# Layer 0's normed input and softmax weights transposed through memory, reads issued when their write has landed

## The chip, the cores and the metric

One core of one Trainium2 chip runs the whole program; the other cores are idle. The metric is the device time of one execution in microseconds (us). The engines of the core are TensorE (PE, with its weight loads listed as PEld), VectorE (DVE), ScalarE (ACT), GpSimd (POOL) and SyncE (SP), which here only issues DMAs. The time before is 4961.98 us, the median of three runs (4956.65 to 4962.49).

## The reference, cut to what matters

Four layers work on `x` of 64 graphs, 256 nodes each, 128 features, all with one 256x256 matrix `adj`. Each layer adds its output to `x`. The change is almost wholly in layer 0:

```python
h = jnp.maximum(_layernorm(x, axis=-1), 0.0)       # 64 graphs x 256 nodes x 128
W1, W2 = adj[:, :128], adj[:, 128:]
s1 = jnp.einsum('bkf,ef->bke', h, W1)              # receivers
s2 = jnp.einsum('bkf,ef->bke', h, W2)              # senders
pre = s1[:, :, None, :] + s2[:, None, :, :] + b_lin
hh = jnp.where(pre >= 0, pre, 0.2 * pre)           # 64 x 256 x 256 x 256 values
e = jnp.einsum('bije,e->bij', hh, a) + adj
attn = jax.nn.softmax(e, axis=2)
x = x + jax.nn.sigmoid(jnp.einsum('bij,bjf->bif', attn, h))
```

Layers 1 to 3 are much smaller: a gated aggregation over `adj` (layer 1), an attention with a tanh and an exponential (layer 2), and five steps of a gated recurrent update (layer 3), which multiply 256x256 by 256x128 and 128x128 by 128x256 per graph.

## The kernel before, in words

**Tiling.** The 64 graphs are cut into 34 groups (line 15): 1, 1, thirty groups of 2, 1, 1. A block is 128 nodes, so a group of two graphs has G = 4 blocks and a tile of it is 128 partitions x 512 values. Everything is float32.

**Layer 0's pairs.** For every graph, receiver i and feature e the kernel needs the maximum of a sender row and a number of the receiver. `Pairs.make` (line 681) writes these in tiles `r` of 4 x 2 x 256 values (one batch: 8 receivers, 128 features, 256 senders). Three engines share the batches: ACT (line 720) and POOL (line 725) make one 128x256 piece an instruction, DVE (line 702) a whole batch (128x2048) or half of one (128x1024). PE multiplies a batch by a window of weights (line 786) into the graph's scores `e_ps`: four matmuls of 512 columns for a batch of the first kind, eight of 256 columns for one of the second. When at least SPARE = 5 batches wait for PE, DVE adds the second half of the features to a batch in place (`merge`, line 744). Two merged batches take 8 such additions and spare PE one batch.

**Order.** The order of all engines is written when the program is built. A planner (line 1359 on) keeps a clock for PE, DVE, ACT and POOL (`Model`), adds a cost for each recorded instruction, and always records next what can start first. Chains of steps (`Chain`, line 1273) hold the rest of the layers as generators: each `yield` names the engine of the next step, a condition and an earliest time; `paced` chains are also held to one step per `pace` ns. Engines then run their instructions in the recorded order and wait for each other by semaphores.

**Transposes.** Matmuls need some tiles with features on partitions. Layers 1 to 3 send most of them through memory: `crossed` (line 97) records on SP's queue a write of the tile to DRAM and at once a read back in transposed order, 16 bytes at a time (4 values, one per block); the read waits for the write's landing. The planner holds the user of the tile back by `Model.transfer`: TURN = 12500 ns of a serial memory, plus SURE = 7000 ns. Such tiles are laid out as [feature, node, block] (`across`). A few late tiles are transposed by PE (`by_pe`, line 875).

**Layer 0's own transposes.** `head` (line 528) norms a group's `x` (`ln_relu`, line 448), and `transpose_blocks` (line 483) turns it: G transposes on PE and one copy on ACT (line 493) into `h0t`. From `h0t` come `s1` and `s1n` (receivers, lines 545 and 547), a bound through a small DMA round trip (`bounds`, line 552), and per graph `left_ps` and `s2` (`senders`, line 577) and the opening matmul of the scores (`open`, line 750). When a graph's scores are complete, `softmax0` (line 791) takes the row maximum on DVE, the exponential with its row sum on ACT (line 809; the sum is read out by a second instruction of ACT), the reciprocal on DVE (line 815), four transposes of the weights on PE (line 819 on), one copy of them on ACT with a factor 0.5 (line 826), the matmul with `h` (line 831), two tanh on ACT (line 839) and an addition to `x` on DVE.

**SP's queue** takes, in recorded order: the loads of `x` (line 149), the writes and reads of `crossed` (lines 101 and 103), the rows and the bound (lines 571 and 573) and the stores of the result (line 1267).

Of the kernel before, what the change touches and what calls it, by code (L numbers as in the profile page):

```python
# [12 lines left out]
P = 128  # L13
# [11 lines left out]
TURN = 12500  # L25
# [16 lines left out]
class Model:  # L42
# [16 lines left out]
    def transfer(self, e):  # L59

        self.memory = max(self.memory, self.t[e] + 900) + TURN
        return self.memory + SURE
# [3 lines left out]
def kernel(ctx: ExitStack, tc: tile.TileContext, ins: dict, out: bass.AP):  # L66
# [30 lines left out]
    def crossed(src, tag, name, by, bufs=1):  # L97

        shape = [P, src.shape[1], src.shape[2]]
        there = dp.tile(shape, F32, tag="there%d" % src.shape[2], name="there", bufs=3)  # L100
        nc.sync.dma_start(out=there, in_=src)
        t = bp.tile(shape, F32, tag=tag, name=name, bufs=bufs)
        nc.sync.dma_start(out=t, in_=there.rearrange("p f g -> f p g"))
        return t, model.transfer(by)
# [67 lines left out]
    adj_n = fetch([P, 2, N], "adj_n", adj.rearrange("(c p) m -> p c m", p=P), nc.scalar)  # L172
# [66 lines left out]
    def constants0():  # L239
# [125 lines left out]
        dve(1).tensor_copy(left_b, p[:, P + 1 : P + 2])  # L365
        counts["left"] += 1
# [81 lines left out]
    def ln_relu(space, xt, tag, ln, when=None, at=None, across=False):  # L448
# [22 lines left out]
        for g in range(G):  # L471
            if g % 2 == 0:
                yield "act"
            if g == 0:
                shape = [P, P, G] if across else [P, G, P]
                h = space.tile(shape, F32, tag=ln, name=tag, bufs={ap: 3, bp: 1}.get(space))
            act(P, 2, 1).activation(  # L477
                h[:, :, g] if across else h[:, g, :], xt[:, g, :], AF.Relu, bias=shift[:, g : g + 1],
                scale=rstd[:, g : g + 1],
            )  # L480
        return h

    def transpose_blocks(space, src, name, banks, when=None, tag=None, bufs=None):

        yield "pe", when
        G, _, W = sizes(src)
        tp = banks([P, G, P], name + "_ps")
        turn()
        for g in range(G):
            tr(tp[:, g, :], src[:, g, :])  # L490
        yield "act"
        t = space.tile([P, G, P], F32, tag=tag or name, name=name, bufs=bufs)
        act(W).copy(t, tp)  # L493
        return t


    def first_head(xt, to, snd):
# [3 lines left out]
        h_t = yield from transpose_blocks(ap, h, "h0t", psum_h)  # L501
# [50 lines left out]
    def bounds(of):  # L552
# [4 lines left out]
        G = h_t.shape[1]  # L557
        p = psum_h([P, P], "bound_ps")
        model.op("pe", P * 1.676)
        for c in range(G):  # L560
            nc.tensor.matmul(
                p[bass.ts(c, 32), :], lhsT=left_w, rhs=h_t[:, c, :], start=True, stop=True
# [14 lines left out]
    def senders(b, of, to):  # L577

        h_t = flat(of["h_t"][:, 2 * b : 2 * b + 2, :])
        if "bound" not in of:  # L580
# [3 lines left out]
        mm(p, lhsT=left2, rhs=h_t, start=True, stop=True)  # L584
# [3 lines left out]
            adj_l, p, of["bound"][:, 2 * b : 2 * b + 1], adj_n[:, 0, :], ALU.min, ALU.add  # L588
# [6 lines left out]
        for ec in range(2):  # L595
            mm(p[:, ec, :], lhsT=w_p[:, 1, bass.ts(ec, P)], rhs=h_t, start=True, stop=True)
# [5 lines left out]
    class Pairs:  # L602
# [5 lines left out]
        def __init__(self, g, b, of, snd):  # L608
# [8 lines left out]
            self.s1n_v = of["s1n"][:, :, bass.ts(b, N)].rearrange(  # L617
                "p c (k g t) -> p c g k t", k=2, g=4
            )
            self.s1n_b = of["s1n"][:, :, bass.ts(b, N)].rearrange(  # L620
                "p c (k g t) -> p c k g t", k=2, g=4
            )
# [49 lines left out]

        def nodes(self, batch, g2):
# [3 lines left out]
                (g, k, self.b * N + 32 * g + t + (P + k if two else k * P))  # L677
# [3 lines left out]
        def make(self, who):  # L681
# [10 lines left out]
            if who == "dve":  # L692
# [4 lines left out]
                if batch["two"]:  # L697
                    s1n = self.s1n_b[:, ec, 1, 2 * g2 : 2 * g2 + n, t : t + 2].unsqueeze(3)
# [92 lines left out]
    def softmax0(g, b, of, e_ps, snd):  # L791
# [27 lines left out]
        for jc in range(2):  # L819
            for ic in range(2):  # L820
                tr(
                    pt_ps[:, jc, bass.ts(ic, P)], pm[:, ic, bass.ts(jc, P)]
                )
# [50 lines left out]

    def by_pe(h, tag, bufs=None, when=None, space=bp):

# [595 lines left out]
```

## Time and profile before

| what | value |
|---|---|
| runs | 4956.65, 4961.98, 4962.49 us |
| profiled execution | 4962.75 us, of which the profile's span is 4960.9 us |
| PE busy | 4923.5 us (99%) |
| ACT busy | 4873.2 us (98%) |
| DVE busy | 4841.8 us (98%) |
| POOL busy | 4756.8 us (96%) |
| granted TensorE clock | 0.999 |
| DMA queue of SP | 121.35 MB in 3429712 packets, 56.5% of 16 engines' time |
| transposes through memory of 256 KB | 104 (`hf`) + 86 (`h`), each a write and a read |

"Busy" is the time in which at least one instruction of the engine is under way. Instructions overlap on PE and ACT, so their cost is read from the distance between the starts (or ends) of neighbours rather than from the duration of one. The list of groups gives, for each line and form, the number of instructions, the busy time of the group, and the mean duration of one. A matmul of the program stands as two instructions in the profile. The DMA share in the view by windows is a sum over packets and can exceed 1 (1.82 is seen).

### The profile page before, as it was taken

Reading aid. Unit: us, or ns where it says so; the run is one execution under the profiler, and the core shown is the slowest. Engines: PE = TensorE matmul, PEld = TensorE weight load, DVE = VectorE, ACT = ScalarE, POOL = GpSimd, SP = SyncE. Lnnn points to the kernel's source line nnn. Section 1 sums busy time; section 2 is a strip of 40 time slices with the busy share of each in tenths; the row PEclk is TensorE's granted clock in tenths of the full one; section 3 lists DMA queues with packets and bytes.
Section 4 is the critical chain, followed back from the end, with each engine's and each line's share of the span. In section 5 each row is a group of like instructions: output and inputs, shape, how many; then the busy total and the mean of one; then the engine's idle time right before and its main releaser. Section 6 shows DMA issues by size and latency. Waiting matters only on the chain.

```text
span 4960.9 us, 176723 instructions
## 1 busy us (share of the span) xinstructions
PE 4923.5 (99%) x69735; PEld 2389.7 (48%) x69735; DVE 4841.8 (98%) x8229; ACT 4873.2 (98%) x12812; POOL 4756.8 (96%) x10545
## 2 busy tenths in 40 slices
PE   9999999999999999999999999999999999999998
PEld 4454545554454544444445444444454444444444
DVE  9999999999999999999999999999999999999994
ACT  8999999999999999999999999999999999999994
POOL 8999999999999999999999999999999999999981
PEclk9999999999999999999999999999999999999999
DMA  0357576777676776866757656656666555542310
GB/s 21 10 17 23 25 30 27 32 32 30 30 33 27 32 32 28 34 27 30 33 27 30 30 27 32 32 26 32 30 32 32 26 31 30 29 26 12 19 9 8
DMA packets 3431090, 132.92 MB, mean 27 GB/s; under 512 B 3369201, under 2 KB 3405937, under 8 KB 3430257
## 3 DMA queue, kind: packets, MB, share of 16 engines
q1 hardware_dynamic: 3429712, 121.35, 56.5%
q8 instruction: 547, 8.96, 0.9%
q14 instruction: 287, 2.34, 0.3%
q10 hardware_dynamic: 544, 0.26, 0.0%
HBM read 61.48 MB, written 60.10 MB: 25 GB/s over the span
## 4 chain that ended last, share of the span: by engine, by line
PE 85%; ACT 7%; DVE 5%; POOL 1%; issue 1%; DMA 0%; ACTq 0%; DVEq 0%; POOLq 0%
PE e_ps L786 53%; PE gate_ps L128 8%; PE hv_ps L128 5%; ACT r L720 5%; PE m_ps L128 5%; PE s_ps L128 3%; DVE r L702 3%; PE o_ps L128 2%; PE e_ps L128 2%; PE rc_ps L128 1%; POOL r L725 1%; PE rsum_ps L128 1%; DVE r L744 1%; PE e_ps L135 1%; PE th_ps L128 1%
## 5 line engine op out<-in xcount | busy, mean ns | idle before, releaser
L725 POOL TENSOR_SCALAR r<-s,s1n 128x256 f32<-128x256 f32 x9920 | 4509.6, 543 | 47.1 <-PE e_ps L786 21.1
L720 ACT ACTIVATE r<-s_act,s 128x256 f32<-128x256 f32 x9768 | 4421.0, 1212 | 1.1 <-PE e_ps L786 1.0
L786 PE MATMUL e_ps<-r,a_win 128*32 128x256 f32 (+1 forms) x41040 | 3323.2, 464 | 9.1 <-DVE r L702 7.5
L702 DVE TENSOR_TENSOR r<-s_ps,s1n 128x2048 f32<-128x2048 f32 (+1 forms) x1367 | 2417.3, 1804 | 0.0
L786 PEld LDWEIGHTS e_ps<-r,a_win 128*32 128x32 f32 x41040 | 1394.2, 110 | 1603.7 <-issue 825.0
L744 DVE SCALAR_TENSOR_TENSOR r<-s_ps,s1n,r 128x256 f32<-128x256 f32 x4056 | 1671.5, 472 | 0.8 <-POOL r L725 0.3
L477 ACT ACTIVATE h<-xt,bsh,brs 128x128 f32<-128x128 f32 x512 | 417.6, 1318 | 7.5 <-POOL bsh L470 7.5
L720 ACT ACTIVATE r<-s,s 128x256 f32<-128x256 f32 x512 | 319.2, 1416 | 0.0
L128 PE MATMUL m_ps<-adj_q,hn 128*32 128x256 f32 x4096 | 252.1, 380 | 1.6 <-ACT hn L1140 1.6
L128 PEld LDWEIGHTS m_ps<-adj_q,hn 128*32 128x32 f32 x4096 | 160.8, 132 | 89.4 <-issue 25.4
L1192 ACT ACTIVATE gate_ps<-gate_ps,bz 128x512 f32<-128x512 f32 (+1 forms) x140 | 202.5, 1447 | 0.0
L1194 ACT ACTIVATE hv_ps<-hv_ps,bh 128x512 f32<-128x512 f32 (+1 forms) x140 | 200.9, 1435 | 0.0
L1180 ACT ACTIVATE m_ps<-gate_ps,br 128x512 f32<-128x512 f32 (+1 forms) x140 | 194.0, 1386 | 0.0
L1176 ACT COPY m_t<-m_ps 128x512 f32<-128x512 f32 (+1 forms) x140 | 184.7, 1319 | 0.0
L128 PE MATMUL gate_ps<-m_t,t_w_w 128*32 128x512 f32 (+1 forms) x1360 | 174.8, 568 | 0.4 <-ACT m_t L1090 0.3
L128 PE MATMUL hv_ps<-rh,u_th 128*32 128x512 f32 (+1 forms) x1360 | 170.9, 567 | 1.3 <-DVE rh L1103 1.3
L128 PE MATMUL gate_ps<-m_t,w_t 128*32 128x512 f32 (+1 forms) x1360 | 171.1, 568 | 0.6 <-ACT m_ps L1100 0.6
L128 PE MATMUL hv_ps<-m_t,t_w_w 128*32 128x512 f32 (+1 forms) x1360 | 171.0, 567 | 0.0
L809 ACT ACTIVATE pm<-e_ps,nmax 128x256 f32<-128x256 f32 x128 | 145.7, 1138 | 2.4 <-DVE nmax L800 2.4
L128 PE MATMUL gate_ps<-hf,u_t 128*32 128x512 f32 (+1 forms) x1088 | 139.8, 567 | 0.0
L128 PE MATMUL s_ps<-h0t,w_p 128*32 128x256 f32 (+1 forms) x1568 | 138.9, 445 | 0.6 <-ACT h0t L493 0.5
L940 ACT ACTIVATE th_ps<-th_ps,a_src 128x256 f32<-128x256 f32 x128 | 134.8, 1053 | 1.5 <-PE th_ps L128 1.5
(223 smaller groups left out, 4612.8 us busy)
## 6 DMA issues: line engine op xcount, KB each, us to landing
there<-hf SPq DMA_DIRECT2D x104, 256.0 KB
hn<-there SPq DMA_DIRECT2D x104, 256.0 KB
there<-h SPq DMA_DIRECT2D x86, 256.0 KB
h_t<-there SPq DMA_DIRECT2D x60, 256.0 KB
xt<-in_x_dram SPq DMA_DIRECT2D x30, 256.0 KB
out_dram<-xt SPq DMA_DIRECT2D x30, 256.0 KB
h3t<-there SPq DMA_DIRECT2D x26, 256.0 KB
row<-rows SPq DMA_DIRECT2D x128, 0.5 KB
```

The source lines that it names most:

```text
L128: nc.tensor.matmul(out[bass.ts(c, 32)], lhsT=lhsT[:, bass.ts(c, 32)], rhs=rhs, **flags)
L477: act(P, 2, 1).activation(h[:, :, g] if across else h[:, g, :], xt[:, g, :], AF.Relu, bias=shift[:, g : g + 1], scale=rstd[:, g : g + 1],)
L702: nc.vector.tensor_tensor(r[:, 2 * g2 : 2 * g2 + n, :, :], s2[:, ec : ec + 1, :].unsqueeze(1).to_broadcast([P, n, 2, N]), s1n.to_broadcast ...
L720: nc.scalar.activation(r[:, g, ic, :], s2[:, ec, :], AF.Relu, bias=s1[:, ec, i : i + 1])
L725: nc.gpsimd.tensor_scalar(r[:, g, ic, :], s2[:, ec, :], FLT_MAX, s1n[:, ec, i : i + 1], ALU.min, ALU.max,)
L744: nc.vector.scalar_tensor_tensor(r[:, g, ic, :], self.own("dve")[:, 1, :], self.of["s1n"][:, 1, i : i + 1], r[:, g, ic, :], ALU.max, ALU.add,)
L786: nc.tensor.matmul(to, lhsT=a_win[:, sign, 31 - t : 63 - t], rhs=of, start=False, stop=self.over, skip_group_check=True,)
L809: act(N, 1, more=119).activation(pm[:, ic, :], e_ps[:, ic, :], AF.Exp, bias=nmax[:, ic : ic + 1], scale=-1.0, accum_out=rs[:, ic : ic + 1],)
L1176: act(W).copy(m_t, m_ps)
L1180: act(W, 1).activation(m_ps, g_ps, AF.Tanh, bias=br, scale=0.5)
L1192: act(W, 1).activation(g_ps, g_ps, AF.Tanh, bias=bz, scale=0.5)
L1194: act(W, 1).activation(hv_ps, hv_ps, AF.Tanh, bias=bh)
```

## The change

`h0t` and the softmax weights `pt` are now made by `crossed`, which can put its tile in another pool. `h0t` goes through memory for every group but the first, `pt` for all graphs of groups 0 to 31 (62 of 64). `crossed` records the write and leaves the read in a list; the planner records the read when its own clock has reached the write's landing (LANDED = 2700 ns after the write's turn) and only then knows when the tile is due (FETCH = 10300 ns of the serial memory, and SURE as before).

All tiles of `h` now have the layout [feature, node, block], and with it `h0t`, `s1`, `s1n` and the weights: a graph of a group of two takes two of every four values. The exponential's two halves are written with every second value each (`pm`), without a row sum. `h` has a 129th column of 2.0, set on POOL, so that the weights' matmul yields twice the row sum beside the weighted sum; the reciprocal is taken of that after the matmul, and the factor 0.5 falls away. The columns of `adj` that are added to the scores are kept in the matching order (`adj_j`). The planner also gets other places for the last layer's exclusive use of two banks (`Home.enter` and `leave`, step by step instead of for the whole layer), a pace of 1700 instead of 2300 for the two lanes of layer 3, and a `due` that is raised when a step is looked at rather than when it is queued.

```diff
...
 MEMORY = (7000, 30000)
-TURN = 12500
+STORE = 1300
+LANDED = 2700
+FETCH = 10300
 SURE = 7000
...
-        self.memory = max(self.memory, self.t[e] + 900) + TURN
+        self.memory = max(self.memory, self.t[e] + 900) + STORE
+        return self.memory + LANDED - STORE
+    def fetch(self, landed):
+        self.memory = max(self.memory, landed) + FETCH
         return self.memory + SURE
...
-    def crossed(src, tag, name, by, bufs=1):
-        shape = [P, src.shape[1], src.shape[2]]
+    def crossed(src, tag, name, by, bufs=1, space=bp):
+        shape = [P, P, src.shape[2]]
         there = dp.tile(shape, F32, tag="there%d" % src.shape[2], name="there", bufs=3)
-        nc.sync.dma_start(out=there, in_=src)
-        t = bp.tile(shape, F32, tag=tag, name=name, bufs=bufs)
-        nc.sync.dma_start(out=t, in_=there.rearrange("p f g -> f p g"))
-        return t, model.transfer(by)
+        nc.sync.dma_start(out=there, in_=src[:, 0:P, :])
+        t = space.tile(shape, F32, tag=tag, name=name, bufs=bufs)
+        due = [None]
+        landed = model.transfer(by)
+        def read():
+            nc.sync.dma_start(out=t, in_=there.rearrange("p f g -> f p g"))
+            due[0] = model.fetch(landed)
+        reads.append((landed, read))
+        return t, due
...
     a_col = column("L0_gnn_a", nc.scalar)
-    adj_n = fetch([P, 2, N], "adj_n", adj.rearrange("(c p) m -> p c m", p=P), nc.scalar)
+    adj_n = bp.tile([P, 2, N], F32, tag="e_t", name="adj_n", bufs=2)
+    fetch([P, 2, N], "adj_n", adj.rearrange("(c p) m -> p c m", p=P), nc.scalar, adj_n)
+    adj_j = constant([P, 2, P, 2], "adj_j")
+    by_j = adj_j.rearrange("p c q m -> p c (q m)")
     blin = column("L0_gnn_b_lin")
...
         dve(1).tensor_copy(left_b, p[:, P + 1 : P + 2])
+        dve(2 * N).tensor_copy(
+            adj_j.rearrange("p c q m -> p c m q"), adj_n.rearrange("p c (m q) -> p c m q", m=2)
+        )
         counts["left"] += 1
...
             if g == 0:
-                shape = [P, P, G] if across else [P, G, P]
-                h = space.tile(shape, F32, tag=ln, name=tag, bufs={ap: 3, bp: 1}.get(space))
+                wide = P + 1 if space is ap else P
+                h = space.tile([P, wide, G], F32, tag=ln, name=tag, bufs={ap: 3, bp: 1}.get(space))
             act(P, 2, 1).activation(
-                h[:, :, g] if across else h[:, g, :], xt[:, g, :], AF.Relu, bias=shift[:, g : g + 1],
+                h[:, 0:P, g], xt[:, g, :], AF.Relu, bias=shift[:, g : g + 1],
                 scale=rstd[:, g : g + 1],
             )
+        if space is ap:
+            pool(80).memset(h[:, P : P + 1, :], 2.0)
         return h
-    def transpose_blocks(space, src, name, banks, when=None, tag=None, bufs=None):
+    def by_pe(h, tag, bufs=None, when=None, space=bp, banks=None):
         yield "pe", when
-        G, _, W = sizes(src)
-        tp = banks([P, G, P], name + "_ps")
+        if when is free_a:
+            using_a.append(tag)
+        G = h.shape[2]
+        tp = (banks or psum_a)([P, P, G], "h_t_ps")
         turn()
         for g in range(G):
-            tr(tp[:, g, :], src[:, g, :])
+            tr(tp[:, :, g], h[:, 0:P, g])
         yield "act"
-        t = space.tile([P, G, P], F32, tag=tag or name, name=name, bufs=bufs)
-        act(W).copy(t, tp)
+        t = space.tile([P, P, G], F32, tag=tag, name="h_t", bufs=bufs)
+        act(P * G).copy(t, tp)
         return t
+    def free_a():
+        return not using_a
...
         h = yield from ln_relu(ap, xt, "h0", "h0", at=LANDS)
-        h_t = yield from transpose_blocks(ap, h, "h0t", psum_h)
+        h_t = yield from by_pe(h, "h0t", None, None, ap, psum_h)
         to.update(h=h, h_t=h_t)
...
         h = yield from ln_relu(ap, xt, "h0", "h0")
-        h_t = yield from transpose_blocks(ap, h, "h0t", psum_h, settled)
+        h_t, at = crossed(h, "h0t", "h0t", "act", None, ap)
         to.update(h=h, h_t=h_t)
+        yield "pe", None, at
         if counts["left"] > 0:
...
-        h_t = flat(of["h_t"][:, 2 * b : 2 * b + 2, :])
+        h_t = of["h_t"][:, :, 2 * b : 2 * b + 2]
         if "bound" not in of:
...
         p = psum_h([P, N], "left_ps")
-        mm(p, lhsT=left2, rhs=h_t, start=True, stop=True)
+        mm(pairs(p), lhsT=left2, rhs=h_t, start=True, stop=True)
         yield "dve", None, of["bound_at"]
...
         dve(N, 1).scalar_tensor_tensor(
-            adj_l, p, of["bound"][:, 2 * b : 2 * b + 1], adj_n[:, 0, :], ALU.min, ALU.add
+            adj_l, p, of["bound"][:, 2 * b : 2 * b + 1], by_j[:, 0, :], ALU.min, ALU.add
         )
...
+        def at(self, q, k):
+            return q * self.of["h_t"].shape[2] + 2 * self.b + k
         def nodes(self, batch, g2):
...
             return [
-                (g, k, self.b * N + 32 * g + t + (P + k if two else k * P))
+                (g, k, self.at(32 * g + t + (k if two else 0), 1 if two else k))
                 for g in (2 * g2, 2 * g2 + 1) for k in range(2)
...
                 mm(
-                    self.e_ps[:, ic, :], lhsT=v2_rep,
-                    rhs=flat(self.of["h_t"][:, 2 * b : 2 * b + 2, :]),
+                    pairs(self.e_ps[:, ic, :]), lhsT=v2_rep,
+                    rhs=self.of["h_t"][:, :, 2 * b : 2 * b + 2],
                     start=(ic == 0), stop=False, skip_group_check=True,
...
             dve(N, more=10).tensor_tensor_reduce(
-                e_ps[:, ic, :], e_ps[:, ic, :], adj_n[:, 1, :] if ic else snd["adj_l"], -1.0, FLT_MAX,
+                e_ps[:, ic, :], e_ps[:, ic, :], by_j[:, 1, :] if ic else snd["adj_l"], -1.0, FLT_MAX,
                 ALU.add, ALU.min, nmax[:, ic : ic + 1],
...
             if ic == 0:
-                pm = ap.tile([P, 2, N], F32, tag="pm", name="pm", bufs=1)
-                rs = sp.tile([P, 2], F32, tag="rs", name="rs")
-            act(N, 1, more=119).activation(
-                pm[:, ic, :], e_ps[:, ic, :], AF.Exp, bias=nmax[:, ic : ic + 1], scale=-1.0,
-                accum_out=rs[:, ic : ic + 1],
-            )
-        yield "dve"
-        rh = sp.tile([P, 2], F32, tag="rh", name="rh")
-        dve(2).reciprocal(rh, rs)
-        yield "pe"
-        pt_ps = e_ps
-        turn()
-        for jc in range(2):
-            for ic in range(2):
-                tr(
-                    pt_ps[:, jc, bass.ts(ic, P)], pm[:, ic, bass.ts(jc, P)]
-                )
-        yield "act"
-        pt = ap.tile([P, 2, N], F32, tag="pt", name="pt", bufs=1)
-        act(2 * N, table=1).activation(pt, pt_ps, AF.Copy, scale=0.5)
-        yield "pe"
-        o_ps = e_ps[:, :, 0:P]
+                pm = ap.tile([P, P, 2, 2], F32, tag="pm", name="pm", bufs=1)
+            act(N, 1).activation(
+                pm[:, :, :, ic], pairs(e_ps[:, ic, :]), AF.Exp, bias=nmax[:, ic : ic + 1],
+                scale=-1.0,
+            )
+        src = pm.rearrange("p q j i -> p q (j i)")
+        if g in BY_MEMORY:
+            pt, at = crossed(src, "pt", "pt", "act", 1, ap)
+            yield "pe", None, at
+        else:
+            yield "pe"
+            tp = flat(e_ps).rearrange("p (q g) -> p q g", q=P)
+            turn()
+            for k in range(4):
+                tr(tp[:, :, k], src[:, :, k])
+            yield "act"
+            pt = ap.tile([P, P, 4], F32, tag="pt", name="pt", bufs=1)
+            act(2 * N).copy(pt, tp)
+            yield "pe"
+        o_ps = e_ps[:, :, 0 : P + 1]
         for ic in range(2):
...
                 mm(
-                    o_ps[:, ic, :], lhsT=pt[:, jc, bass.ts(ic, P)], rhs=h[:, b * 2 + jc, :],
+                    o_ps[:, ic, :], lhsT=pt[:, :, 2 * jc + ic], rhs=h[:, :, b * 2 + jc],
                     start=(jc == 0), stop=(jc == 1),
                 )
+        yield "dve"
+        rh = sp.tile([P, 2], F32, tag="rh", name="rh")
+        dve(2, more=120).reciprocal(rh, o_ps[:, :, P])
+        o_ps = o_ps[:, :, 0:P]
         for ic in range(2):
...
+        def free(self):
+            return self.banks or not inside
+        def enter(self):
+            if not self.banks:
+                inside.append(self)
+        def leave(self):
+            if not self.banks:
+                inside.remove(self)
         def bank(self, shape, name):
...
         for step in range(STEPS):
-            yield "pe"
+            yield "pe", home.free
+            home.enter()
             m_ps = home.bank([P, W], "m_ps")
...
                 return None
+            if isinstance(self.earliest, list):
+                if self.earliest[0] is None:
+                    return None
+                self.earliest = self.earliest[0]
+            self.due = max(self.due, self.earliest)
             return max(
...
     chain1, chain2 = Chain(2200), Chain(2200)
-    lanes = [Chain(2300), Chain(2300)]
+    lanes = [Chain(1700), Chain(1700)]
     chain4, chain5 = Chain(2400), Chain(2400)
...
     sent = [{} for _ in graphs]
-    to_load = []
+    to_load, reads = [], []
     making, multiplying = [], []
...
                     best = (at, e, None)
+        if reads and (best is None or best[0] >= reads[0][0]):
+            reads.pop(0)[1]()
+            continue
         if best is None:
...
         at, what, step = best
...
```

More of the change, by code (lines that the diff above doesn't have):

```diff
@@ L444, in constants1, with ln_relu @@
                 dve(1).tensor_scalar(t, t, scale, None, ALU.mult)
-    def ln_relu(space, xt, tag, ln, when=None, at=None, across=False):
+    def ln_relu(space, xt, tag, ln, when=None, at=None):
         G = xt.shape[1]
@@ L556, in bounds @@
         h_t = of["h_t"]
-        G = h_t.shape[1]
+        G = h_t.shape[2]
         p = psum_h([P, P], "bound_ps")
@@ L561, in bounds @@
             nc.tensor.matmul(
-                p[bass.ts(c, 32), :], lhsT=left_w, rhs=h_t[:, c, :], start=True, stop=True
+                p[bass.ts(c, 32), :], lhsT=left_w, rhs=h_t[:, :, c], start=True, stop=True
             )
@@ L595, in senders @@
         for ec in range(2):
-            mm(p[:, ec, :], lhsT=w_p[:, 1, bass.ts(ec, P)], rhs=h_t, start=True, stop=True)
+            mm(
+                pairs(p[:, ec, :]), lhsT=w_p[:, 1, bass.ts(ec, P)], rhs=h_t, start=True, stop=True
+            )
         yield "act"
@@ L615, in __init__ @@
             self.owned, self.by_act = {}, 0
-            self.s1n_v = of["s1n"][:, :, bass.ts(b, N)].rearrange(
-                "p c (k g t) -> p c g k t", k=2, g=4
-            )
-            self.s1n_b = of["s1n"][:, :, bass.ts(b, N)].rearrange(
-                "p c (k g t) -> p c k g t", k=2, g=4
-            )
+            G = of["h_t"].shape[2]
+            self.s1n_v = of["s1n"].rearrange("p c (g t k) -> p c g k t", g=4, k=G)[
+                :, :, :, 2 * b : 2 * b + 2, :
+            ]
         def more(self):
@@ L697, in make @@
                 if batch["two"]:
-                    s1n = self.s1n_b[:, ec, 1, 2 * g2 : 2 * g2 + n, t : t + 2].unsqueeze(3)
+                    s1n = self.s1n_v[:, ec, 2 * g2 : 2 * g2 + n, 1, t : t + 2].unsqueeze(3)
                 else:
@@ L806, in softmax0 @@
             if ic == 0:
-                pm = ap.tile([P, 2, N], F32, tag="pm", name="pm", bufs=1)
-                rs = sp.tile([P, 2], F32, tag="rs", name="rs")
-            act(N, 1, more=119).activation(
-                pm[:, ic, :], e_ps[:, ic, :], AF.Exp, bias=nmax[:, ic : ic + 1], scale=-1.0,
-                accum_out=rs[:, ic : ic + 1],
-            )
-        yield "dve"
-        rh = sp.tile([P, 2], F32, tag="rh", name="rh")
-        dve(2).reciprocal(rh, rs)
-        yield "pe"
-        pt_ps = e_ps
-        turn()
-        for jc in range(2):
-            for ic in range(2):
-                tr(
-                    pt_ps[:, jc, bass.ts(ic, P)], pm[:, ic, bass.ts(jc, P)]
-                )
-        yield "act"
-        pt = ap.tile([P, 2, N], F32, tag="pt", name="pt", bufs=1)
-        act(2 * N, table=1).activation(pt, pt_ps, AF.Copy, scale=0.5)
-        yield "pe"
-        o_ps = e_ps[:, :, 0:P]
+                pm = ap.tile([P, P, 2, 2], F32, tag="pm", name="pm", bufs=1)
+            act(N, 1).activation(
+                pm[:, :, :, ic], pairs(e_ps[:, ic, :]), AF.Exp, bias=nmax[:, ic : ic + 1],
+                scale=-1.0,
+            )
+        src = pm.rearrange("p q j i -> p q (j i)")
[13 more added lines that the diff above has]
+        o_ps = e_ps[:, :, 0 : P + 1]
         for ic in range(2):
@@ L873, in elu_1 @@
         return mn
-    def by_pe(h, tag, bufs=None, when=None, space=bp):
-        yield "pe", when
-        if when:
-            using_a.append(tag)
-        G = h.shape[2]
-        tp = psum_a([P, P, G], "h_t_ps")
-        turn()
-        for g in range(G):
-            tr(tp[:, :, g], h[:, :, g])
-        yield "act"
-        t = space.tile([P, P, G], F32, tag=tag, name="h_t", bufs=bufs)
-        act(P * G).copy(t, tp)
-        return t
     def pairs(t):
@@ L984, in layer2 @@
         G, NB, W = sizes(x2)
-        h = yield from ln_relu(bp, x2, "h2", "h", across=True)
+        h = yield from ln_relu(bp, x2, "h2", "h")
         if by_memory:
@@ L1141, in layer3 @@
                 hn = hn.rearrange("p (g n) -> p g n", g=G)
-        yield "pe"
+            home.leave()
+        yield "pe", home.free
+        home.enter()
         tp = home.bank([P, W], "y_ps")
@@ L1148, in layer3 @@
         dve(W).tensor_tensor(x3, tp.rearrange("p (g n) -> p g n", g=G), x3, ALU.add)
+        home.leave()
     def layer3_across(x3, lane):
@@ L1156, in tile3 @@
             return bp.tile([P, P, G], F32, tag=name, name=name)
-        hn = yield from ln_relu(bp, x3, "h3" + tag, "hn" + tag, across=True)
+        hn = yield from ln_relu(bp, x3, "h3" + tag, "hn" + tag)
         h, at = crossed(hn, "hf" + tag, "h3t", "act", 2)
@@ L1216, in first_norm @@
     def first_norm(g, xt):
-        h = yield from ln_relu(bp, xt, "h1", "ln", across=True)
+        h = yield from ln_relu(bp, xt, "h1", "ln")
         h_t = at = None
@@ L1221, in first_norm @@
         chain1.add(first_rest(g, xt, h, h_t, at))
-    def free_a():
-        return not using_a
     def first_rest(g, xt, h, h_t, at):
@@ L1237, in second_rest @@
         if g >= len(GROUPS) - 2:
-            hn = yield from ln_relu(rp, xt, "h3", "r", no_tiles, across=True)
+            hn = yield from ln_relu(rp, xt, "h3", "r", no_tiles)
             h_t = yield from by_pe(hn, "r", None, free_a, rp)
@@ L1241, in second_rest @@
             hn = yield from ln_relu(
-                bp, xt, "h3", "hn" + tag, lambda: done3(g - 2), across=True
+                bp, xt, "h3", "hn" + tag, lambda: done3(g - 2)
             )
@@ L1260, in last_rest @@
                 yield "pe", lambda: n == len(graphs) and not (making or doing or multiplying)
-            else:
-                yield "pe", lambda: not inside
-                inside.append(g % 2)
             yield from layer3(xt, hn, h_t, home)
-            if not home.banks:
-                inside.remove(g % 2)
         nc.sync.dma_start(out=of_group(out, g), in_=xt)
@@ L1298, in advance @@
                 self.earliest = self.earliest or 0.0
-                self.due = max(self.due, self.earliest)
                 return
```

## The prediction

> **What bounds the kernel now.** I read the page first, then busy times by windows, then the timelines of PE and SP, then the groups by form.
>
> ```profile
> PE 4923.5 (99%) x69735; PEld 2389.7 (48%) x69735; DVE 4841.8 (98%) x8229; ACT 4873.2 (98%) x12812; POOL 4756.8 (96%) x10545
> ...
> PE 85%; ACT 7%; DVE 5%; POOL 1%; issue 1%; DMA 0%; ACTq 0%; DVEq 0%; POOLq 0%
> ```
>
> ```profile
> 120.00:4720.00 4600.00, 4590.86 (x65080) 2234.04 (x65076) 4562.93 (x7715) 4599.22 (x12111) 4532.04 (x10033) 1.00 0.62 28
> 4720.00:4961.00 241.00, 223.70 (x3092) 105.46 (x3084) 168.39 (x371) 166.58 (x415) 119.01 (x270) 0.98 0.07 8
> ```
>
> Columns of the second: stretch, its length, then busy PE, PEld, DVE, ACT, POOL, clock, DMA share, GB/s. All four engines are full from 120 to 4720 us; only the ends have air. Busy overstates PE and ACT, so I take distances between starts:
>
> ```profile
> 1499.49 0.66 PE L135 MATMUL e_ps<-ident,pm 128*128 128x128 f32 x4
> 1500.07 1.07 PE L128 MATMUL s_ps<-h0t,w_p 128*32 128x512 f32 x8
> ...
> 1504.46 1.06 PE L128 MATMUL e_ps<-h,pt 128*32 128x128 f32 x32
> 1505.33 0.61 PE L128 MATMUL left_ps<-h0t,left 128*32 128x256 f32 x8
> ...
> 1508.35 1.05 PE L128 MATMUL s_ps<-h0t,w_p 128*32 128x256 f32 x16
> 1509.21 1.10 PE L128 MATMUL s_ps<-g_t,h_t 128*32 128x256 f32 x16
> 1510.13 1.05 PE L786 MATMUL e_ps<-r,a_win 128*32 128x256 f32 x16
> ```
>
> Four transposes hold PE 0.58 us (median 0.586). Sixteen matmuls of 256 columns hold it 0.86 (0.863, eight of 512 columns 0.858), but 0.92 when the moving tile is read two values in four (`s_ps<-g_t`). With these spacings the scores (L786) take 16384/8 x 0.858 + 24656/16 x 0.863 = 3087 us, all transposes some 98, all other matmuls 1677: PE streams 4862 of 4961 us. Of the other 99, 7.5 lie before the first matmul, 38 in the first and last 124 us, and only 54 in between. The same count by ends leaves ACT, DVE and POOL about 1 us idle in each 124 us of the middle. So this is a four-way tie.
>
> **The change, part by part.** The built order of instructions gives counts; durations are rows of before.
>
> *ACT.* Gone: 62 copies of `pt` (starts 0.488 apart) 30.3 us, 30 copies of `h0t` at 0.476 and 4 of half size at 0.26, 15.3, and the row sums: exponential and accumulator end 0.367 + 0.091 apart, a bare tanh of that size (L940) 0.344, so 128 x 0.114 = 14.6. Added: 52 pieces (L720) at 0.365, 19.0. Net -41. Writes of one value in four cost no throughput: of L477's stores the strided ones end up to 0.145 late, and the next instruction catches up (0.222 instead of 0.365).
>
> *DVE and POOL.* These rows carry it:
>
> ```profile
> L725 POOL TENSOR_SCALAR r<-s,s1n 128x256 f32<-128x256 f32 x9920 | 4509.6, 543 | 47.1 <-PE e_ps L786 21.1 <-DVE v_rep L319 9.2 <-issue 1.1
> ...
> L702 DVE TENSOR_TENSOR r<-s_ps,s1n 128x2048 f32<-128x2048 f32 x761 | 1719.3, 2277 | 0.0
> L744 DVE SCALAR_TENSOR_TENSOR r<-s_ps,s1n,r 128x256 f32<-128x256 f32 x4056 | 1671.5, 472 | 0.8 <-POOL r L725 0.3 <-ACT r L720 0.2
> ...
> L702 DVE TENSOR_TENSOR r<-s_ps,s1n 128x1024 f32<-128x1024 f32 x606 | 719.0, 1210 | 0.0
> ```
>
> DVE: 432 fewer additions at 0.392 (spacing of ends) -169.3, 46 more whole batches at 2.194 +100.9, 27 more halves at 1.127 +30.4, one `adj_j` +0.7: -37. The reciprocal moves from SBUF (0.153) to PSUM (0.162 in L1035): nothing. POOL: 96 fewer pieces at 4509.6/9920 = 0.455, -43.6; 34 memsets at 0.152 (L1004), +5.2: -38.
>
> *PE.* Gone: four transposes each for 62 `pt` and 30 `h0t`, two each for three: 62 x 0.586 + 31.5 x 0.587 = -54.8. Back: 432 fewer additions are 54 batches that PE multiplies itself, 54 x 0.863 = +46.6. A 129th column: `o_ps` takes 0.885 for 32 instead of 0.873, +0.8 over 64 graphs. Moving tiles of `h0t` now read two in four: per graph 0.061 for `s2`, 0.061 for the opening, 0.024 for `left_ps` (`th_ps`, read so already, 0.456 against 0.432): +9.3.
>
> The unknown is the moving `h` of `o_ps`, now one value in four; no moving tile of before is read so. Below: nothing, as the strided weights of `hv_ps` (0.873 for 32, like contiguous ones). Above: weight loads of 128 values go from 141 to 209 ns (`h0t_ps`, `y_ps`), 68 ns; if each of the 32 matmuls paid it, four abreast, 32 x 68/4 = 0.54 us a graph, 35 us in all. A gain has no reason. I take twice the pair row's penalty (3.8 ns for 256 values that share a stride in pairs, so about 3.8 for 128 single ones), 32 x 3.8 = 0.12 us, +7.8: it is a moving read, as this is. PE: +10 in all, 0 to +37.
>
> [...]
>
> *Memory.*
>
> ```profile
> 1622.53 0.36 SPq L103 DMA_DIRECT2D h_t<-there  x1
> 1622.94 9.94 SPq L101 DMA_DIRECT2D there<-hf  x1
> 1634.66 0.36 SPq L103 DMA_DIRECT2D hn<-there  x1
> ```
>
> A read of 256 KB blocks SP's next issue for 9.9 us; from read to read 12.1 us. A group of two (about 154 us) has 7 such pairs now, 85 us, and 10 then, 121 us, or 79%. The traffic itself is hidden under the engines. Issuing the read 2.7 us after the write, with other issues in between, removes SP's wait of 2.1 us (239.8/112), which costs nobody anything now. Behind a waiting SP instruction stand all later reads: the row and the bound (L571, L573) now stand between writes and reads of three tiles. Behind a late `pt` or `h0t` on PE stand the next batches; when the 12 buffers of `r` are full, ACT, POOL and DVE stand too. The planner leaves 7 us; by the read's last packet PE's first use came a median 7 to 11 us later in before. `e_ps` is held 20 us longer (2.7 + 10.3 + 7), and the graph after next wants it 78 us later: covered, else PE stops for the difference. `pm` and `pt` have one buffer and the same 78 us. The reciprocal now stands between matmul and tanh; a step of a paced chain, beside the batches. The pace and `Home` move steps, not work; the last group's chain after the last pairs (100 us) has the same instructions but two (581 PE rows for 575): nothing.
>
> *Sum.* ACT, DVE and POOL lose 37 to 41 us: with their waits unchanged the span is 4961 - 38 = 4923. PE: 4862 + 10 + 45.5 at the ends = 4917 plus its waits in the middle, 54 now. As the other three run ahead of PE by 38 + 10 us over the run, its waits for just-made tiles should go; I keep about a quarter, 15: 4932. PE becomes the engine that sets the end. With 1.9 us outside the span (4962.75 - 4960.9), and 0.8 for the profiled run above the median: 4933.
>
> **Rivals.**
>
> *PE was the wall alone (0.14).* For: 85% of the chain. Then its 54 us of waits stay: 4862 + 10 + 45.5 + 54 + 1 = 4972; with three quarters of them 4959: no difference. Against: the other three show no idle middle either, so they do not wait for PE now.
>
> *Transfers come late: slower (0.14).* Place: PE at the first matmul on `pt`, `h0t` or `hn`. The planner counts 11.6 us a pair where the chip took 12.1, and no time for `x`, the stores, rows and bound: 5 + about 8 us a group against 7 us of margin. If two of ten tiles are 1.2 us late, 32 groups lose 77 us less what the buffers take up: about 4990. It decides from 1.2 us a group (39 us). For: 79% of the queue's time. Against: 33 us a group of free time in which the queue catches up.
>
> *The strided `h` halves PE's rate at `o_ps`: slower (0.09).* 64 x 0.87 (the row's 0.873 once more) instead of 0.12, +48: 4981. It decides from 0.75 us a graph. Against: no strided row of before pays more than 0.54 by the count above.
>
> *PE's added costs are nothing and its waits go too (0.05).* 4862 - 8 + 45.5 + 5 + 1 = 4906.
>
> **How the numbers follow.** The forecast's own range, 4915 to 4952, has 0.58: its low end has no waits, its high end the 35 us price with half these waits. About 0.2% (10 us) can be told from no change. Faster 0.58 + 0.05, same 0.14, slower 0.14 + 0.09. For 8 in 10 the range reaches from 4909 into the slower cases, to 4985.
>
> **What would show it.** Right: L744 near 3624 x 0.392, four-transposes rows of `pm` and `h0t` gone but for two graphs, PE's idle middle under 30 us, POOL or ACT waiting for `e_ps` more than now (21.1 and 1.0 us), `o_ps` some 1.0 us for 32. Wrong: PE waiting for `pt<-there`, `h0t<-there` or `hn<-there`; `o_ps` above 1.6 us for 32; ACT, DVE and POOL as busy as before while the time falls.

## The result, and the profile after

| | before | after |
|---|---|---|
| median of the runs (us) | 4962.23 (4956.65 to 4962.55, 4 runs) | 5016.05 (5015.94 to 5016.53, 4 runs) |
| profiled execution, its span (us) | 4962.75, 4960.9 | 5015.94, 5014.2 |
| ratio, 95% interval | | 1.0111 [1.0094, 1.0129] |

The change made the kernel 1.1% slower: 53.8 us over before, where 29 us less were forecast. From the page of the changed kernel, busy times and the chain that ended last:

```profile
PE 4973.2 (99%) x70225; PEld 2687.2 (54%) x70225; DVE 4819.2 (96%) x7871; ACT 4860.8 (97%) x12641; POOL 4720.0 (94%) x10483
...
PE 95%; DVE 2%; POOL 1%; ACT 1%; issue 1%; DMA 0%; DVEq 0%; ACTq 0%; POOLq 0%
```

DVE, ACT and POOL are busy for less time than before, PE for 50 us more, and the chain is now 95% PE. So PE has become the bound, as forecast, but at the wrong height. The timeline of PE shows what it does in that time (start, duration, line, instructions). I read the distance between the starts of neighbouring rows:

```profile
2014.35 2.06 PE L142 MATMUL e_ps<-h,pt 128*32 128x129 f32 x32
2016.20 8.81 PE L817 MATMUL e_ps<-r,a_win 128*32 128x512 f32 x112
```

`o_ps` (the weights' matmul with `h`, whose output lies in the bank `e_ps`) takes 32 matmuls a graph, and they hold PE 1.85 us (about 1.86 as the median over the run); the same row of before was 0.873. That is 0.97 us more for each of the 60 graphs in groups of two. The four single graphs read `h` at a step of two values and pay under 0.1 us each, so the stride costs some 59 us in all. What PE waits for (engine and line that waits, for whom; us in total, times, longest):

```profile
PE e_ps L142 <- DVE xt L874: 5.1, 2, 3.4
PE hn_ps L149 <- DVE hf L1160: 5.1, 3, 2.1
PE before_ps L142 <- DVE a_abs L278: 3.9, 1, 3.9
PE e_ps L817 <- POOL r L756: 3.0, 6, 1.0
PE e_ps L817 <- DVE r L733: 2.6, 5, 1.0
```

No tile from memory (`pt`, `h0t`, `hn`) is among the longest waits, so PE does not stand still for a late transfer. The first line is a score bank held too long, twice.

The start differs too. Busy times by windows of before and after (stretch, its length, busy PE, PEld, DVE, ACT and POOL with instructions, clock, DMA share, GB/s):

```profile
80.00:100.00 20.00, 19.97 (x256) 9.38 (x248) 19.99 (x28) 20.00 (x56) 19.17 (x44) 1.00 0.02 2
100.00:120.00 20.00, 20.00 (x304) 9.48 (x305) 19.93 (x23) 20.00 (x56) 19.83 (x45) 1.00 0.01 2
```

```profile
80.00:100.00 20.00, 17.99 (x191) 6.25 (x188) 17.40 (x31) 10.08 (x26) 13.03 (x30) 1.00 0.38 24
100.00:120.00 20.00, 19.02 (x239) 9.55 (x241) 18.74 (x11) 17.24 (x48) 19.65 (x45) 1.00 0.79 31
```

ACT loses 13 us and POOL 6 between 80 and 120 us. The timelines of POOL and ACT after name the releasers (in brackets: idle time before the row, and who ended it):

```profile
79.80 0.92 POOL L756 TENSOR_SCALAR r<-s,s1n 128x256 f32<-128x256 f32 x2
87.69 13.20 POOL L756 TENSOR_SCALAR r<-s,s1n 128x256 f32<-128x256 f32 x29 [6.97 <-ACT s L628]
...
87.01 0.59 ACT L628 COPY s<-s_ps 128x512 f32<-128x512 f32 x1 [4.33 <-PE s_ps L142]
102.76 1.00 ACT L497 ACTIVATE h<-xt,bsh,brs 128x128 f32<-128x128 f32 x2 [7.80 <-POOL bsh L490]
```

That `s` belongs to the second graph. Its `h0t` now goes out to memory and back when there is not yet other work: the read is issued at 48.9 us and PE first uses the tile at 71.0, where before it used PE's own transpose at 59.6. POOL stands still for 7 us and ACT for 4.3; ACT's further 7.8 are for `bsh`, a small tile of the next group's norm that POOL makes. How much of the delay is the transfer, and how much the margin that the planner adds to it, was not separated.

**Where the 53 us of span are.** For each kernel I took the spacings of PE's groups, priced every matmul at the undisturbed spacing of its form ("stream"), and split the rest. Such a count is good to a few us. All in us, from the two traces:

| part of PE's time | before | after | forecast of the difference | measured |
|---|---|---|---|---|
| stream (transposes, batches, 129th column) | 4862 | 4854 | -7 | -8 |
| moving `h` of `o_ps` | 0 | 59 | +8 | +59 |
| moving `h0t` in pairs (`s2`, opening, `left_ps`) | 0 | 7 | +9 | +7 |
| moving `h0t` in `bound_ps` | 0 | 7 | not counted | +7 |
| waits in the middle | 54 | 23 | -39 | -31 |
| excess in the first 124 us | 15 | 27 | 0 | +12 |
| excess in the last 124 us | 23 | 29 | 0 | +6 |
| sum | | | -29 | +52 |

The three terms that were worked out from rows of before (stream, pairs, waits) hold within 8 us each. One price is wrong by a factor of some eight, `bound_ps` was missed, and the start and the end were taken at nothing.

### The profile page after: what moved, and what is told of

Its sections match the earlier page's. It is cut to its first block, busy times and chain, and to the rows that moved or that the text cites. A ratio compares the mean times of both kernels' runs of the same rounds, so it can differ in the third digit from the quotient of the medians.

```text
span 5014.2 us, 177258 instructions
## 1 busy us (share of the span) xinstructions
PE 4973.2 (99%) x70225; PEld 2687.2 (54%) x70225; DVE 4819.2 (96%) x7871; ACT 4860.8 (97%) x12641; POOL 4720.0 (94%) x10483
## 4 chain that ended last, share of the span: by engine, by line
PE 95%; DVE 2%; POOL 1%; ACT 1%; issue 1%; DMA 0%; DVEq 0%; ACTq 0%; POOLq 0%
PE e_ps L817 59%; PE gate_ps L142 8%; PE hv_ps L142 6%; PE m_ps L142 5%; PE e_ps L142 3%; PE s_ps L142 3%; PE o_ps L142 2%; PE rc_ps L142 2%; POOL r L756 1%; DVE r L733 1%; PE rsum_ps L142 1%; ACT r L751 1%; PE th_ps L142 1%; PE y_ps L142 1%; PE xh_ps L142 1%
## 5 line engine op out<-in xcount | busy, mean ns | idle before, releaser
L756 POOL TENSOR_SCALAR r<-s,s1n 128x256 f32<-128x256 f32 x9824 | 4468.5, 480 | 99.8 <-PE e_ps L817 61.8
L751 ACT ACTIVATE r<-s_act,s 128x256 f32<-128x256 f32 x9820 | 4025.3, 774 | 8.3 <-PE e_ps L817 8.3
L817 PE MATMUL e_ps<-r,a_win 128*32 128x256 f32 (+1 forms) x41904 | 3386.1, 463 | 5.9 <-POOL r L756 3.0
L733 DVE TENSOR_TENSOR r<-s_ps,s1n 128x2048 f32<-128x2048 f32 (+1 forms) x1440 | 2552.3, 1814 | 3.6 <-PE e_ps L817 2.8
L817 PEld LDWEIGHTS e_ps<-r,a_win 128*32 128x32 f32 x41904 | 1608.4, 110 | 1460.6 <-issue 790.5
L775 DVE SCALAR_TENSOR_TENSOR r<-s_ps,s1n,r 128x256 f32<-128x256 f32 x3624 | 1496.5, 477 | 1.8 <-POOL r L756 0.9
L497 ACT ACTIVATE h<-xt,bsh,brs 128x128 f32<-128x128 f32 x512 | 315.3, 875 | 19.9 <-POOL bsh L490 12.3
L488 POOL TENSOR_TENSOR brs<-bve,neg_half 128x4 f32<-128x4 f32 (+1 forms) x136 | 134.0, 985 | 0.0
L142 PE MATMUL e_ps<-h,pt 128*32 128x129 f32 x2048 | 133.2, 407 | 0.7 <-ACT pt L855 0.7
L477 DVE BATCH_NORM_STATS2 bst<-xt 128x6 f32<-128x128 f32 x512 | 122.5, 282 | 2.0 <-DMA xt<-in_x_dram 1.6
L1227 ACT ACTIVATE hv_ps<-hv_ps,bh 128x512 f32<-128x512 f32 (+1 forms) x140 | 123.3, 880 | 0.0
```

The costliest lines, as they stand in the source:

```text
L142: nc.tensor.matmul(out[bass.ts(c, 32)], lhsT=lhsT[:, bass.ts(c, 32)], rhs=rhs, **flags)
L477: dve(P).bn_stats(st[:, g, :], xt[:, g, :])
L488: pool(1085).tensor_tensor(rstd, ve, neg_half[:, 0:G], ALU.pow)
L497: act(P, 2, 1).activation(h[:, 0:P, g], xt[:, g, :], AF.Relu, bias=shift[:, g : g + 1], scale=rstd[:, g : g + 1],)
L733: nc.vector.tensor_tensor(r[:, 2 * g2 : 2 * g2 + n, :, :], s2[:, ec : ec + 1, :].unsqueeze(1).to_broadcast([P, n, 2, N]), s1n.to_broadcast ...
L751: nc.scalar.activation(r[:, g, ic, :], s2[:, ec, :], AF.Relu, bias=s1[:, ec, i : i + 1])
```

## The experiments

Each table or line gives the median, and its difference to the kernel before run on the same chip; the medians of that kernel lie between 4955.7 and 4962.9 us on the five chips used, so times from different chips are not compared directly. Square brackets hold the 95% interval of the ratio to it.

### Is it the strided read of h? (e1, e2, e3, e5)

`e1_still_h`: the changed kernel, but `o_ps` reads a constant contiguous tile in place of `h`.

```diff
...
-                    o_ps[:, ic, :], lhsT=pt[:, :, 2 * jc + ic], rhs=h[:, :, b * 2 + jc],
+                    o_ps[:, ic, :], lhsT=pt[:, :, 2 * jc + ic], rhs=flat_h,
```

> The change with one edit: the weights' matmul reads a constant contiguous tile of 129 columns instead of h, so its products are not the reference's; the order of all instructions is the same. Theory A (the moving tile read one value in four costs PE double): o_ps falls from 1.85 to 0.885 us for 32 matmuls, PE streams 64 x 0.97 = 62 us less, ACT, DVE and POOL become the bound again: 4940 to 4965 us. Rival B (transfers that come late, or SP's queue, hold PE): all transfers are the same, so 5010 to 5016.

4967.8 us, +5.2, 1.0011 [1.0002, 1.0021]: 48.6 us of the 53.8 are gone, just above the range expected by A and far from B's. `o_ps` takes 0.880 us. The transfers are all still there, so they are not what cost the time.

`e2_before_strided`: the reverse. The kernel before, with only this changed: the 128 values that `o_ps` reads of `h` are one in four (one in two for the four single graphs).

```diff
...
-                    rhs=h[:, b * 2 + jc, :],
+                    rhs=flat(h).rearrange("p (q k) -> p q k", k=h.shape[1])[:, :, b * 2 + jc],
```

> The kernel before with one edit: the weights' matmul reads 128 values of h at a step of four (of two for the four single graphs), so its products are not the reference's; no transfer is added. A: o_ps goes from 0.873 to about 1.85 us for 32 on 60 graphs, 59 us more on PE; as PE had 54 us of waits in its middle and loses perhaps half of them, 4990 to 5020. B: 4960 to 4966.

5006.72 us, +44.1, 1.009 [1.0075, 1.0105]. PE is held 57 us longer there (60 x (1.815 - 0.873), and 0.05 for each single graph) and the kernel pays 44: the rest went into waits that PE had anyway. Neither memory nor order was touched, so the strided read alone does it.

`e3_steps`: the changed kernel with the step of the read going 1, 2, 3, 4 values from graph to graph (1 for the single graphs).

```diff
...
-                    rhs=h[:, :, b * 2 + jc],
+                    rhs=stepped(h, 2 * g + b),
```

> The change, with the weights' matmul reading columns of h at a step of 1, 2, 3 or 4 values, by graph (two-graph groups with an even number: 1 and 2, odd: 3 and 4; single graphs 1), so its products are not the reference's. [...] Rival (any step but 1 costs the same double): 0.885, 1.85, 1.85, 1.85. Time about 4985 by A, 5000 by the rival.

One run, 4986.66 us: 2 us above the forecast of A, by which the price grows with the step, and 13 under the rival's. PE's timeline in the order of steps 4, 1, 2, 3:

```profile
2005.86 2.05 PE L142 MATMUL e_ps<-h,pt 128*32 128x129 f32 x32
2007.70 8.81 PE L817 MATMUL e_ps<-r,a_win 128*32 128x512 f32 x112
...
2065.71 1.09 PE L142 MATMUL e_ps<-h,pt 128*32 128x129 f32 x32
2066.59 2.79 PE L817 MATMUL e_ps<-r,a_win 128*32 128x256 f32 x40
...
2159.33 1.19 PE L142 MATMUL e_ps<-h,pt 128*32 128x129 f32 x32
2160.32 7.96 PE L817 MATMUL e_ps<-r,a_win 128*32 128x512 f32 x104
...
2217.51 1.70 PE L142 MATMUL e_ps<-h,pt 128*32 128x129 f32 x32
2218.90 2.03 PE L817 MATMUL e_ps<-r,a_win 128*32 128x256 f32 x24
```

Distances of starts 1.84, 0.88, 0.99, 1.39; medians over the run 1.856, 0.880, 0.969, 1.40 us. A step of two values costs 10%; three and four cost 0.46 us per value of step (1.40 / 3 = 0.467, 1.856 / 4 = 0.464). The price of a pair step therefore says nothing of the price of a step of four. The rival, that any step but one costs the same double, fell with 0.969 and 1.40.

`e5_reads_later`: the kernel before with only the third part of the change, the reads recorded when their writes have landed.

> The kernel before with the third part of the change alone: a read is issued when its write has landed by the planner's clock, with the planner's new times, and the due time raised when a step is looked at. A: no engine's work changes and SP's waits cost nobody anything: 4955 to 4970. B (the queue's order matters by itself): a change of over 10 us either way.

4962.66 us, +0.1, 1.0001 [0.9992, 1.001]: this part is neutral.

### The start and the bound (e4, e7, e8, e10, e15, e16)

`e4_two_copies`: `h` in contiguous blocks of 129 values for `o_ps`, and a second copy on DVE (0.823 us a group of two, 26 us in all) for the way through memory.

```diff
...
-        h_t, at = crossed(h, "h0t", "h0t", "act", None, ap)
+        h_x = bp.tile([P, P, G], F32, tag="ln", name="h_x", bufs=1)
+        dve(W).tensor_copy(h_x.rearrange("p f g -> p g f"), h[:, :, 0:P])
+        h_t, at = crossed(h_x, "h0t", "h0t", "dve", None, ap)
...
```

> The change, but h of layer 0 is laid out block by block, so that the weights' matmul reads it contiguously, and DVE makes a second copy in the other layout for the way through memory (33 copies, about 0.6 us each). A: PE loses 62 us, DVE gains 20, shared among three engines: 4940 to 4970. B: 5010 or more. The result is the reference's.

4970.84 us, +8.2, 1.0017 [1.0008, 1.0027]: just over the range.

`e7_bound_flat` is e4 with contiguous columns in `bounds` (`rhs=flat(h_t)[:, bass.ts(c, P)]`, and the small read of the bound sorts the numbers); `e16_bound_alone` is the changed kernel with that edit alone.

> The two-copies version (4970.8 us), with the bound's four matmuls over contiguous columns of h0t instead of one value in four; the same numbers come out in another order, and the small read of the bound sorts them. A (PE sets the pace there): 33 x 0.22 = 7 us less, 4960 to 4966. Rival (PE has air for it): 4969 to 4973.

> The changed kernel with contiguous columns in bound alone, 0.218 us instead of 0.440 for its 8 matmuls, 33 times, 7.3 us of PE. If PE alone sets the end: 5 to 9 us under the changed kernel (45 to 49 over before). If the other engines take it up, as e4_two_copies and e7_bound_flat say (8.2 and 8.4 over before): within 3 us of it.

e7: 4964.03 us, +8.4, 1.0016 [1.0007, 1.0026]. It looks 7 us faster than e4, but its chip runs the kernel before 7 us faster too: against that, nothing. e16: 5012.52 us, +56.6, 1.0115 [1.0098, 1.0132]. The row fell from 0.440 to 0.218 us in both, and no gain of the 7.3 us of PE is seen in either; the intervals are some 5 to 8 us wide on either side, so a few us can't be excluded. In e16 the rival's forecast holds (2.8 us from the changed kernel, within 3).

`e8_second_graph` is e4 with the second group's `h0t` transposed by PE as before; `e15_second_alone` is the changed kernel with that alone undone; `e10_both_mended` is e8 with e7's bound.

```diff
...
+        if xt is xts[1]:
+            h_t = yield from by_pe(h, "h0t", None, settled, ap, psum_h)
+            at = None
...
```

> The two-copies version (4970.8 us), with the second group's h0t made by PE instead of through memory. A (three engines stand up to 8 us near 85 and 104 us because the second graph's tile comes late): 8 to 20 us less, 4951 to 4963. Rival (the engines catch up later, so nothing is lost there): 4967 to 4973.

> The changed kernel with one part undone: the second group's h0t is transposed by PE again. If that group's lateness at 80 to 105 us costs the run what those engines lose there: 8 to 14 us under the changed kernel (40 to 46 over before). If later slack takes it up: within 4 us of it (50 to 58 over before).

> e8_second_graph and contiguous columns in bound: the whole change without its three costs on PE and at the start. A (costs add up; bound's was 7 us between e4_two_copies and e7_bound_flat): 4942 to 4950, faster than before by 0.2 to 0.4%. B (PE's saving is taken up elsewhere): 4951 to 4957, as e8.

e8: 4953.17 us, -2.5, 0.9996 [0.9986, 1.0005], 10.9 under e7's difference on the same chip. e15: 4997.25 us, +41.3, 1.0083 [1.0068, 1.0098], 12.5 under the changed kernel's difference, in the range. Its windows show the start full again:

```profile
80.00:100.00 20.00, 17.50 (x238) 7.36 (x234) 19.93 (x31) 20.00 (x56) 18.12 (x43) 1.00 0.31 21
100.00:120.00 20.00, 19.36 (x272) 8.33 (x267) 20.00 (x12) 19.41 (x55) 20.00 (x45) 1.00 1.08 34
```

ACT stands at 20.00 and 19.41 of 20, beside 10.08 and 17.24. One tile of 128 KB (this group has one graph) sent the long way at the wrong time costs 11 to 13 us.

e10, the whole change without its three costs: 4956.87 us, -5.7, 0.9988 [0.998, 0.9997], in B's range and not in A's. It is the fastest against before of all that were run, by 0.1%, and its interval only just leaves out no change.

### The parts that were to bring the gain (e6, e9)

`e6_weights_alone`: only `pt` through memory, row sums and late reads; `h` and `h0t` as before.

> The kernel before with one part of the change: the softmax weights through memory, row sums from a 129th column, reads issued when landed; h, h0t and all that reads them stay in blocks, as before. A (the strided moving tiles and the late second graph cost the time, the traffic is hidden): PE -36 + 1, ACT -45, POOL +5, shared: 4938 to 4955. B (traffic or SP's order costs): no gain or slower, 4960 to 4985. The result is the reference's.

4977.04 us, +21.4, 1.0042 [1.0027, 1.0056]: A missed, and the time lies in B's range. But this kernel wrote the exponential one value in four, where the changed kernel writes one in two, which neither reading had priced. The exponential in ACT's trace, before and e6 (duration min/median/max, in ns):

```profile
L809 ACT ACTIVATE pm<-e_ps,nmax x128: 465/1232/1713, 91.2 to 4867.7; 128x256 f32<-128x256 f32 x128
```

```profile
L826 ACT ACTIVATE pm<-e_ps,nmax x128: 672/1345/2472, 90.7 to 4857.0; 128x256 f32<-128x256 f32 x128
```

The minimum rose from 465 to 672, and the distance from the end before to its own end from 0.366 to 0.660 us (the changed kernel: 0.408). Part of that is made up at once: the piece of `r` behind it ends 0.213 us later in e6 and 0.340 in the changed kernel, where such pieces are otherwise 0.365 apart. Counted over both, the exponential costs 0.13 us more than a contiguous one in e6, 17 us over 128, and 0.01 in the changed kernel, under 2 us.

`e9_weights_mended`: the same part of the change with the changed kernel's order of the exponential. It is made from the changed kernel, with `h` in blocks, all `h0t` by PE and contiguous columns in `bounds`, so it also has the new pace, `Home` and the pair reads of `h0t`.

> The softmax weights through memory, the row sums from a 129th column and delayed reads, with h in contiguous blocks, all h0t transposed by PE, contiguous columns in bound, and the exponential in the changed kernel's own order (a step of two values, 0.406 us), where e6_weights_alone wrote at a step of four (0.660). A (e6's miss was its own exponential, some 36 us of ACT): 4940 to 4958. B (the weights' way through memory is no gain by itself): 4965 to 4985, as e6.

4966.95 us, +4.4, 1.0008 [0.9999, 1.0017]: 17 us better than e6 by their differences, in keeping with the 15 us of ACT by which its exponentials are cheaper, but still no gain. The time fits B's range; its reading, that the weights' way through memory brings nothing by itself, is what is left, though the other differences just named may hide a few us. 62 x 0.586 = 36 us of PE's transposes are gone there, and PE's stream is 4861 us as before: the planner gave the time back by merging fewer rows on DVE (3760 additions for 4056, which is 37 batches or 32 us more for PE).

### Is the end, or the balance, what is missing? (e11 to e14)

`e11_both_spare4` and `e12_before_spare4` set `SPARE = 4` for 5 in e10 and in the kernel before: rows are merged sooner, so DVE adds more and PE multiplies less.

> As e10_both_mended, and pairs of rows are merged on DVE when four batches are waiting, not five: some PE batches become additions on DVE. A (PE alone sets the end of the mended kernel, the other engines have 30 us and more to spare): 3 to 15 us under e10. C (all four still tie): equal to e10 within 3 us or above it.

> The kernel before with merging when four batches wait. If its four engines tie, as the prediction read them, no gain: 4957 to 4980. If PE alone was its wall: 4940 to 4952.

e11: 4963.16 us, +0.6, 1.0001 [0.9992, 1.001]; e12: 4975.95, +13.4, 1.0028 [1.0017, 1.0038]. PE's stream fell by 19 us in e11 (4836 beside 4855), and its waits in the middle rose by 26 (66 beside 40, strides counted in both). In e12 PE has 544 rows fewer in the profile, which is 29 us, and its waits in the middle rose by some 42. So PE does not set the time alone, neither in e10 nor in the kernel before. That all four engines tie fits this; which of the others shares the bound was not shown.

`e13_unpaced_end` drops the pace for the last five graphs and `e14_old_pace` puts `lanes` back to `Chain(2300)`, both in e10.

> As e10_both_mended, and the chains drop their pace for the last five graphs, not the last two. After the last matmul of the pairs the traces run on for 95 us in the kernel before, 102 in the changed one, 116 in e10, with 1102, 1108 and 1254 PE matmuls. T (paced steps left over from the groups before are what lengthens the end): under 108 us after the last pair, and 5 to 12 us under e10 (4945 to 4952 beside 4957). U (the last graph's own chain sets the end, whatever is left over): equal to e10 within 3 us.

> As e10_both_mended with the pace of the two layer-3 chains back at 2300 from 1700. If the new pace is what the change needed to keep layer 3 up with the rest: 3 to 20 us above e10 and a longer end. If the pace moves steps and no time, as the prediction had it: equal to e10 within 3 us.

e13: 4965.68 us, +2.8, 1.0005 [0.9996, 1.0015], with 124 us after the last pair instead of 116: 8.5 above e10's difference, so both forecasts missed. e14: 4960.29 us, -2.6, 0.9996 [0.9987, 1.0006], with 108 us after the last pair: a shorter end and yet no shorter time, as PE's waits in the middle rose. It lies 3.1 us above e10's difference, between its two forecasts. Steps taken from the end come back elsewhere. The new places of `Home` were not run by themselves.

## Why the prediction was wrong

**What bounds the kernel: right as far as it was shown.** That PE is not the wall alone is shown by e12 (PE relieved, slower) and e2 (PE's 57 us more cost 44). That all four engines tie is read from their idle times.

**PE's stream: right.** -54.8 + 46.6 + 0.8 = -7 forecast, -8 measured. The pair-strided rows came near the forecast (`s2` 0.911 for 16 where 0.924 was priced, `left_ps` 0.456 for 8).

**The moving `h`: this step failed.** "I take twice the pair row's penalty", 0.12 us a graph, +7.8; measured 0.97, and 59 in all. The upper bound of 35 us was too low as well: it was the price of another kind of read, a load of weights. The rival "the strided `h` halves PE's rate", with 0.09, is what happened: its 0.87 us a graph is 10% under the measured one, and its point of decision (0.75) was passed. Its time, 4981, is 35 us low because it put everything else at the forecast (the table's other rows).

e3 has the price of each step: the 32 matmuls take 0.880 us contiguous, 0.969 at a step of two values, 1.40 at three and 1.856 at four. The rival's 64 x 0.87 is 56 us, and 59 were measured. Carrying the price of a row that reads two values in four (0.924 us for 0.863) over to one that reads one in four was the mistake.

**`bound_ps`: left out.** Its 8 matmuls read `h0t` one value in four as well, 0.440 for 0.218 us; the list of strided readers in the prediction missed it. On the whole no gain from mending it is seen (e7, e16).

**The start: left out.** The prediction weighed late transfers as 7 us of margin against busy groups, and found no late tile, rightly: PE waits for none. But the second group's `h0t` is wanted before any other work can cover it, and there POOL and ACT stand still. e15 prices it at 12 us, e8 at 11.

**ACT, DVE and POOL.** Their counts came as forecast (L775 3624 merges). "Writes of one value in four cost no throughput" holds for the writes of `h`: two of them and the piece behind take 1.13 us from end to end, strided or not (before and e15). It does not hold for 256 values (e6: 0.13 us each, as above); at the changed kernel's step of two this is under 2 us.

**`e_ps` held longer: half right.** PE stops 5.1 us for it at two places. POOL's and ACT's waits on `e_ps` rose as the prediction's list said, to 61.8 and 8.3 us from 21.1 and 1.0 (the lines below are of after). But these are waits for PE's multiplications (`L817`), which free the buffers of `r`: a mark that PE is the bound, and not of a held bank.

```profile
L756 POOL TENSOR_SCALAR r<-s,s1n 128x256 f32<-128x256 f32 x9824 | 4468.5, 480 | 99.8 <-PE e_ps L817 61.8
L751 ACT ACTIVATE r<-s_act,s 128x256 f32<-128x256 f32 x9820 | 4025.3, 774 | 8.3 <-PE e_ps L817 8.3
```

**Reads issued later: right.** e5 is +0.1, with an interval of some 5 us either way.

**What stays open.** Without the three costs the change gives -5.7 us, not the -37 that the prediction's terms would give without its +7.8. 26 us of DVE copies stand in e10 that the change doesn't have. Its PE has 33 us of waits in the middle (15 forecast), and 52 us of excess at both ends (38). e11, e13 and e14 moved time between these and won none, so what the missing 31 us are was not shown. A kernel that keeps `h` contiguous and sends `h0t` through memory without the copy was not tried.

## What to carry to other kernels

Before a tile's layout is turned for one reader, list every reader, and price each by a row with the same step: the cost of a moving tile rose by 10% at a step of two float32 values, by 59% at three and by 111% at four (e3). Look at what a long way through memory meets at the start of the program, where nothing covers it: one tile of 128 KB cost 12 us there by e15 and 11 by e8. And where engines tie, time put on one or taken from it counts for only a part: 57 us on PE cost 44 (e2), and 19 us moved from PE's stream to DVE brought nothing (e11).

## What the hardware showed

- 32 float32 matmuls of 129 columns hold PE 0.880, 0.969, 1.40 and 1.856 us when the moving tile is read at a step of 1, 2, 3 and 4 values (e3). The same step in the weights (`pt`, a step of four values) shows no cost: `o_ps` with a contiguous moving tile takes 0.880 us in e3 and 0.880 to 0.886 in e1 and e4, the 129 columns of `o_ps<-hv,pm` in before 0.885. The load of 32 weight columns itself takes a median 138 ns in the changed kernel and 137 in e3, for 110 in before, hidden beside the matmuls.
- ACT's stores of 256 values slow down by step, and the instruction behind makes up a part. From the end before to the end of the next piece of `r`, an exponential and that piece take 0.74 us at a step of two (after) and 0.87 at a step of four (e6); two contiguous instructions of that size take 0.73 (before, without the reading of the row sum). Pairs of stores of 128 values cost nothing so counted: 1.13 us with the piece behind, contiguous or at a step of four (before).
